# Self-attention of a perceiver block: PSUM in eight single banks taken in turn, scores of a head group in three parts

## The chip, the cores and the metric

The kernel runs on one core of a Trainium2 chip. The time is device microseconds (us) of one execution, as the median of several. The engines are TensorE (PE; its weight loads are shown as PEld), VectorE (DVE), ScalarE (ACT), GpSimd (POOL) and SyncE (SP, which issues DMAs). PSUM, where TensorE writes, has 8 banks of 128 partitions x 512 fp32.

## What is computed

Two batch elements of 512 tokens and 512 features pass through three residual layers: cross-attention over 8192 context rows, causal self-attention, and a mixture of 16 experts (two for each token). Only the self-attention is changed. All weights and activations are fp32. Cut to what matters:

```python
q_amp = softplus(x @ Wq_amp.T);  q_phi = pi * tanh(x @ Wq_phi.T)      # k_amp, k_phi alike; 16 heads of 32
q_amp = q_amp / sqrt(mean(q_amp**2) + eps)                            # per head and token; k alike
scores = (q_amp*cos(q_phi) @ (k_amp*cos(k_phi)).T
          + q_amp*sin(q_phi) @ (k_amp*sin(k_phi)).T) / sqrt(32) * exp(log_scale[head])
attn = softmax(where(causal, scores, -inf))
x = x + (attn @ v) @ Wo.T                                             # x was normalised before the projections
```

## The kernel before

The 16 heads go in NG = 4 groups of four; one group's channels fill 128 partitions, 32 to a head. Tokens are in TB = 4 blocks of P = 128. For each batch element b the kernel has, feature by token, `cs[b,i,u]` and `sn[b,i,u]` (amplitude times cosine and sine; i is 0 for queries and 1 for keys, u a pair of groups).

A score product of a group is, for each head, two fp32 matmuls (cosine and sine, `product`, L1093) that use only the head's 32 rows of TensorE, into a bank of the head's own; four heads, in four quarters of the rows, can run side by side. Each fp32 matmul shows as two instructions in the trace. Other shapes on TensorE: full 128 x 128 (projections, `channels`, L874), and column matmuls with 32 columns of weights for each head (values `weighted`, L1158, and sums `close`, L1188; `columns`, L158, does the same with a full weight cut into four).

Scores are made twice. `score_max` (L1101) makes them query by key for block qt, up to the diagonal; VectorE adds the causal mask to the diagonal block (L1108) and takes the row maxima (L1109). `split` writes the maxima as three bf16 parts (VectorE and POOL), and `max_rows` (L1119) turns them into rows with matmuls on an identity, which VectorE casts (L1130). `score_exp` (L1133) makes the scores key by query for key block kt, subtracts the maxima by a bf16 matmul with `sa.minus` (L1141), ScalarE takes the exponential (L1143), and POOL sets what lies above the diagonal to zero (L1145). `weighted` multiplies by the values, `close` sums the exponentials with a matrix of ones, and VectorE divides: it transposes the sums (L1193), takes the reciprocal, transposes back (L1199) and multiplies (L1200).

PSUM has two pools here: `ps` holds three pairs of banks (tag "s", 128 x 2 x 512), and `ps1` two single banks, "j" (projections, rows of maxima, sums, transposes, router) and "av" (values). So a part of scores for four heads takes two of the three pairs.

The order is written out by hand: instructions run on each engine in the order of the program. `attend(b, fill)` goes through the groups; in group g it makes the exponentials of key blocks x = 0 to 3 and, between them, the maxima of group g + 1 in the order of `ORDER` ([3], [2], [1, 0], []), the values of block x - 1, and in x = 0 the sums and the division of group g - 1. Other work is put at named gaps (`fill`, eight to a group and one after it): in `attend(0)` the amplitudes, logarithms, values and phases of batch element 1, cut into single matmuls; in `attend(1)` the second half of `combine` for element 1 and the pieces of `route(0)` (normalisation, transposes, router, ranks of tokens). `first_maxima(b)` makes the maxima of group 0 ahead of it; the four outputs of element 0 (`output`, L1246) stand at the start of `attend(1)`, those of element 1 after it.

Before the attention lies a preparation: values of element 0, the last output tiles of the cross-attention (`finish`, L158 and L482) with the statistics of the normalisation behind them on VectorE, four turns (transposes through bank "j", L142, copied by ScalarE, L143), the raw phases of element 1 (L874), `root` and `combine` for element 0. After it come the rest of `route`, the experts and the output.

The cross-attention ahead of all this already takes its eight PSUM banks singly and in turn.

Of the kernel before, what the change touches and what calls it, by code (L numbers as in the profile page):

```python
# [20 lines left out]
P = 128  # L21
# [21 lines left out]
def perceiver_kernel(ctx: ExitStack, tc: tile.TileContext, a, out: bass.AP):  # L43
# [91 lines left out]
    def turn(ps, pstag, src, dst, copy):  # L135

        if pstag == "s":
            pt = ps.tile([P, 2, 4, P], F32, tag=pstag, name="pt")[:, 0]
        else:
            pt = ps.tile([P, 4, P], F32, tag=pstag, name="pt")  # L140
        for c in range(4):
            nc.tensor.transpose(pt[:, c, :], src[:, c * P : (c + 1) * P], ident)  # L142
        copy(dst, pt)  # L143

    def layernorm(ps, pstag, b, xnT, keep=None):

        for i, xn in enumerate(norm_tiles(b, keep)):
            turn(ps, pstag, xn, xnT[:, :, i * P : (i + 1) * P], nc.scalar.copy)

    def by_chunk(t):  # L150

        return [t[:, c, :] for c in range(ND)]

# [14 lines left out]
    def cross_attention(tail):  # L168

        with ExitStack() as st:  # L170
            wp = st.enter_context(tc.tile_pool(name="xa_w", bufs=1))
            sm = st.enter_context(tc.tile_pool(name="xa_sm", bufs=2))

            ps = st.enter_context(tc.tile_pool(name="xa_ps", bufs=1, space=PSUM))
            turns = [0]

            def bank(at=None):

                if at is None:
                    at, turns[0] = turns[0], turns[0] + 1  # L180
                return ps.tile([P, S], F32, tag=f"s{at % 8}", name="s")
# [304 lines left out]
            def finish(b, ps, tag, qts, after=None):  # L486

                po = ps.tile([P, 2, D], F32, tag=tag, name="po")
                for k, qt in enumerate(qts):
                    finish_tile(b, acc, qt, po[:, k, :], after)  # L490

# [104 lines left out]
            return lambda ps, tag, after: [finish(B - 1, ps, tag, (qt, qt + 1), after) for qt in range(0, TB, 2)]  # L596
# [274 lines left out]
    def channels(pz, w, g, xT, cc=range(ND)):  # L871

        for c in cc:
            nc.tensor.matmul(pz, w[c][:, g * P : (g + 1) * P], xT[:, c, :], start=(c == 0), stop=(c == ND - 1))  # L874
# [12 lines left out]
    def xattn_tail(k):  # L887


        def channels(pz, w, g, xT):  # L890
            for c in range(ND):
                columns(pz, w[c][:, g * P : (g + 1) * P], xT[:, c, :], c == 0, c == ND - 1)
# [86 lines left out]
    def self_attention(finish_cross, mo_w):  # L979
        with ExitStack() as st:  # L980
            wp = st.enter_context(tc.tile_pool(name="sa_w", bufs=1))
            sm = st.enter_context(tc.tile_pool(name="sa_sm", bufs=2))
            ps = st.enter_context(tc.tile_pool(name="sa_ps", bufs=3, space=PSUM))
            ps1 = st.enter_context(tc.tile_pool(name="sa_ps1", bufs=1, space=PSUM))

            def values(b, h, copy):

                if h == 0:
                    vals[b] = b8("v", (P, TB, D))
                pv = ps.tile([P, 2, D], F32, tag="s", name="pv")  # L990
                for k in range(2):
                    i = 2 * h + k
                    for c in range(ND):
                        nc.tensor.matmul(  # L994
                            pv[:, k, :], xnT[b][:, c, i * P : (i + 1) * P], sa.wv[c], start=(c == 0), stop=(c == ND - 1)
                        )
                copy(vals[b][:, 2 * h : 2 * h + 2, :], pv)

            def value(b, i):

                pv = []

                def piece(c):
                    if c == 0:
                        pv.append(ps1.tile([P, D], F32, tag="j", name="pv"))
                    nc.tensor.matmul(
                        pv[0], xnT[b][:, c, i * P : (i + 1) * P], sa.wv[c], start=(c == 0), stop=(c == ND - 1)
                    )
                    if c == ND - 1:
                        nc.vector.tensor_copy(vals[b][:, i, :], pv[0])  # L1010

                return [lambda c=c: piece(c) for c in range(ND)]
# [17 lines left out]
            def root(b):  # L1030

                pq = ps1.tile([P, S], F32, tag="j", name="pss")
# [36 lines left out]
            def raw_phase(b, i, u):  # L1069
                pz = ps.tile([P, 2, S], F32, tag="s", name="pz")  # L1070
                for k in range(2):
                    channels(pz[:, k, :], sa.wphi[i], 2 * u + k, xnT[b])
                cs[b, i, u] = m4("phi")
                nc.scalar.copy(cs[b, i, u], pz)

            def combine(b, rs, i, u):

                pb = ps.tile([P, 2, S], F32, tag="s", name="pb")
                for k in range(2):
                    q = slice((2 * u + k) * HD, (2 * u + k + 1) * HD)  # L1080
                    nc.tensor.matmul(
                        pb[:, k, :], sa.back[q, i].rearrange("p j d -> p (j d)"), rs[q, :], start=True, stop=True
                    )
                z = amp[b, i, u]
                nc.vector.tensor_tensor(z, z, pb, ALU.mult)
# [3 lines left out]
            def product(s, b, g, j, own, lhs_at, other, rhs_at, stop):  # L1089

                r = slice(j * HD, (j + 1) * HD)
                for n, f in enumerate((cs, sn)):
                    nc.tensor.matmul(  # L1093
                        s,
                        f[b, own, g // 2][r, g % 2, lhs_at],
# [72 lines left out]
            def first_maxima(b):  # L1168
                oT[b] = b8("soT")
                cm = sm.tile([P, TB, 4], F32, tag="scm", name="scm")  # L1170
                for qts in ORDER:
                    for qt in qts:
                        score_max(b, 0, qt, cm)
# [260 lines left out]
```

## Time and profile before

| | us |
|---|---|
| median of 3 runs (lowest, highest) | 3122.87 (3122.15, 3124.74) |
| the profiled execution | 3127.96 |
| its span, first to last instruction | 3126.3 |
| TensorE busy in the span | 2967.6 (95%) |
| VectorE, ScalarE, POOL busy | 2024.2 (65%), 1384.2 (44%), 2168.0 (69%) |
| granted TensorE clock, mean | 0.971 |
| cross-attention | to about 2580 |
| self-attention with its preparation | 2580 to 2962 |
| rest of the route, experts, output | 2962 to 3126.3 |

A program's profile gives for each instruction its engine, its line of the kernel, start and length, and what ended an idle time before it ("<-DVE scm L1109": that VectorE instruction released it). A matmul's end is modelled, so busy time of TensorE includes matmuls that run slower than they could. The granted clock is the share of TensorE's full clock that the chip let through; it is given for windows of time.

### The profile page before, as it was taken

What the parts mean: (1) busy time and instruction counts of PE and PEld (TensorE: products, weight loads), DVE (VectorE), ACT (ScalarE), POOL (GpSimd) and SP (SyncE); (2) the same over time, 40 slices, a digit from 0 to 9 for tenths busy, and PEclk for the clock granted to TensorE, in tenths of its full rate; (3) what the DMA queues carried; (4) which work ended last, traced back from release to release, by engine and by line L of the source; (5) the groups of instructions that cost most, each with busy time, mean ns of one, the idle gap of its engine ahead of it and who ended that gap; (6) DMA issues with size and microseconds to landing.
All of it is one profiled execution on the core that took longest, in us unless ns stands there. A gap on an engine that the chain in (4) does not pass through costs nothing.

```text
span 3126.3 us, 62064 instructions
## 1 busy us (share of the span) xinstructions
PE 2967.6 (95%) x26687; PEld 1158.9 (37%) x26687; DVE 2024.2 (65%) x3337; ACT 1384.2 (44%) x2550; POOL 2168.0 (69%) x861
## 2 busy tenths in 40 slices
PE   7999999999999999999999999999999989889875
PEld 3333333333333333333333333333333323344464
DVE  2667776767777677756677776777777656465522
ACT  1345444555555555435555545555544454242211
POOL 1488989898988889968889888989887730010012
PEclk9999999999999999999999999999999999899878
DMA  3000000000000000000000000000000010010274
GB/s 138 1 3 15 10 15 10 23 1 23 4 21 8 16 8 17 15 16 15 10 15 10 15 10 15 10 15 3 2 1 28 28 52 17 1 48 28 89 244 147
DMA packets 47364, 89.51 MB, mean 29 GB/s; under 512 B 4320, under 2 KB 22768, under 8 KB 47088
## 3 DMA queue, kind: packets, MB, share of 16 engines
q1 hardware_dynamic: 39824, 69.26, 6.9%
q0 software_dynamic: 2784, 8.41, 0.9%
q10 hardware_dynamic: 4480, 7.87, 0.8%
q8 instruction: 209, 3.42, 0.5%
q14 instruction: 67, 0.55, 0.1%
HBM read 77.13 MB, written 8.39 MB: 27 GB/s over the span
## 4 chain that ended last, share of the span: by engine, by line
PE 90%; DVE 6%; DMA 1%; issue 1%; ACT 1%; POOL 0%; ACTq 0%; DVEq 0%; POOLq 0%
PE s L158 26%; PE s L375 17%; PE s L440 15%; PE s L388 14%; PE s L407 3%; PE p L1093 3%; PE pz L874 2%; PE ph L794 2%; PE s L467 2%; PE s L310 1%; PE spo L1246 1%; PE po L811 1%; DVE cm L397 1%; PE pv L994 1%; PE spa L1188 1%
## 5 line engine op out<-in xcount | busy, mean ns | idle before, releaser
L576 POOL TENSOR_TENSOR es<-es,e 128x2048 f32<-128x2048 f32 x374 | 1700.2, 4546 | 80.3 <-ACT e L409 63.3
L409 ACT ACTIVATE e<-s 128x512 f32<-128x512 f32 x2048 | 1057.5, 602 | 1116.3 <-PE s L407 1113.3
L397 DVE TENSOR_REDUCE cm<-s 128x1 f32<-128x512 f32 x2048 | 1270.9, 683 | 315.6 <-PE s L375 315.5
L375 PE MATMUL s<-k,qT 32*128 32x512 f32 x4096 | 591.4, 641 | 3.7 <-DVE cm L397 3.7
L388 PE MATMUL s<-qT,k 32*128 32x512 f32 x4096 | 555.6, 595 | 7.6 <-ACT e L409 6.8
L440 PE MATMUL s<-e,v 128*32 128x512 f32 x4096 | 498.2, 604 | 12.6 <-DVE cm L397 11.5
L576 POOL TENSOR_TENSOR es<-e 128x2048 f32<-128x2048 f32 x63 | 286.1, 4541 | 226.5 <-ACT e L409 226.5
L158 PE MATMUL s<-wkv,ctx 128*32 128x512 f32 x3072 | 369.9, 602 | 7.5 <-DVE cm L397 7.2
L158 PE MATMUL s<-ctx,wkv 128*32 128x512 f32 x3072 | 357.2, 599 | 3.5 <-DVE cm L397 3.1
L388 PEld LDWEIGHTS s<-qT,k 32*128 32x128 f32 x4096 | 282.8, 185 | 188.2 <-issue 104.1
L455 DVE TENSOR_TENSOR acc<-acc,s 128x512 f32<-128x512 f32 (+1 forms) x359 | 207.9, 604 | 141.0 <-PE s L440 140.4
L375 PEld LDWEIGHTS s<-k,qT 32*128 32x128 f32 x4096 | 164.7, 183 | 333.7 <-issue 256.9
L440 PEld LDWEIGHTS s<-e,v 128*32 128x32 f32 x4096 | 107.6, 109 | 333.6 <-DVE cm L397 171.6
L407 PE MATMUL s<-rows,mb 4*128 4x512 bf16 x2048 | 217.9, 377 | 0.0
L351 DVE SCALAR_TENSOR_TENSOR k<-s,kf,m 128x512 f32<-128x512 f32 x128 | 96.1, 751 | 177.8 <-PE s L158 177.8
L158 PEld LDWEIGHTS s<-ctx,wkv 128*32 128x32 f32 x3072 | 87.4, 110 | 239.3 <-issue 156.1
L158 PEld LDWEIGHTS s<-wkv,ctx 128*32 128x32 f32 x3072 | 87.2, 110 | 224.6 <-issue 130.4
L1145 POOL TENSOR_SCALAR_AFFINE_SELECT e<-e 128x512 f32<-128x512 f32 x32 | 22.0, 687 | 212.0 <-ACT e L1143 212.0
L366 ACT COPY v<-s 128x512 f32<-128x512 f32 x128 | 75.0, 586 | 119.8 <-PE s L158 96.8
L463 DVE TENSOR_TENSOR acc<-acc,s 128x1024 f32<-128x1024 f32 x56 | 68.4, 1221 | 69.9 <-ACT s L462 69.9
L407 PEld LDWEIGHTS <-mb 4*128 4x128 bf16 x2048 | 68.3, 93 | 106.2 <-issue 105.6
L1093 PE MATMUL p<-phi 32*128 32x384 f32 (+3 forms) x512 | 79.6, 521 | 13.1 <-DVE scm L1109 7.6
(261 smaller groups left out, 1909.6 us busy)
## 6 DMA issues: line engine op xcount, KB each, us to landing
ctx<-in_ctxT_dram SPq DMA_DIRECT2D x48, 512.0 KB, 3.7
wg<-in_L_ffn_w_gate_dram SPq DMA_DIRECT2D x16, 512.0 KB, 4.9
wf<-in_L_ffn_w_fc_dram SPq DMA_DIRECT2D x16, 512.0 KB, 5.6
wp<-in_L_ffn_w_proj_dram SPq DMA_DIRECT2D x16, 512.0 KB, 5.3
results<-res ACTq DMA_DIRECT2D x32, 128.0 KB, 3.4
xs<-in_x_dram SPq DMA_DIRECT2D x2, 1024.0 KB, 6.5
m<-in_mask_BxS_bf_dram SPq DMA_DIRECT2D x16, 128.0 KB, 3.1
w_wq_phiT<-in_wq_phiT_dram SPq DMA_DIRECT2D x2, 1024.0 KB, 5.1
```

The lines of the kernel that those rows point to most:

```text
L158: nc.tensor.matmul(out[q], lhsT[:, q], rhs, start=start, stop=stop)
L351: nc.vector.scalar_tensor_tensor(k[:, keys], bank, kf[:, g, b : b + 1], mask_tiles[i][:, keys], ALU.subtract, ALU.mult)
L366: nc.scalar.copy(v[:, kt % (NKT // 2), :], bank)
L375: nc.tensor.matmul(s, qT(chunks[i][0], g, r, slice(qt * P, (qt + 1) * P)), k_tiles[n][r, hf * S : (hf + 1) * S], start=True, stop=True,)
L388: nc.tensor.matmul(s, k_tiles[n][r, keys], qT(chunks[i][0], g, r, slice(0, S)), start=True, stop=False)
L397: nc.vector.tensor_reduce(cms[g][chunks[i][1] % 2][:, qt, j : j + 1, hf], ss[j], AX.X, ALU.max)
L407: nc.tensor.matmul(ss[j], bias_tiles[i][r4, keys], rows[r4, :], start=False, stop=True)
L409: nc.scalar.activation(e[:, j, :], ss[j], AF.Exp)
L440: nc.tensor.matmul(av[j * HD : (j + 1) * HD, :], v_tiles[i][kt // (NKT // 2)][:, kt % (NKT // 2), h * HD : (h + 1) * HD], e[:, j, :], star ...
L455: nc.vector.tensor_tensor(dst, dst, src, ALU.add)
L576: nc.gpsimd.tensor_tensor(es, first if kt == 1 else es, e, ALU.add)
L1093: nc.tensor.matmul(s, f[b, own, g // 2][r, g % 2, lhs_at], f[b, other, g // 2][r, g % 2, rhs_at], start=(n == 0), stop=stop and n == 1,)
```

## The change

- **PSUM.** The pools `ps` and `ps1` of the self-attention give way to one pool with eight tags, each a single bank, and `Ring` hands them out strictly in turn (0, 1, ... 7, 0, ...). Everything takes its bank there: scores, projections, values, sums, rows of maxima, transposes. The cross-attention's own counter becomes the same class.
- **Parts.** The scores of a group come in three parts of four banks: block 3 (512 columns), block 2 (384), and blocks 1 and 0 in the same bank (256 and 128 beside each other); so for the exponentials, with key blocks 0, 1, and 2 with 3. Causal add, maximum and exponential are one instruction per head in place of one per two heads. The matmuls of a part are written with the function (cosine, sine) outermost and the heads inside.
- **Order.** The maxima run four parts ahead of the exponentials (`AHEAD`), across groups, and stand next to them: maxima, exponentials, then other work. The values and sums of a group stand together after its third part, first blocks 0 and 1, then, after the next group's rows and a gap, blocks 2 and 3; the division follows at once.
- **Fills.** Projections, values and outputs are whole (16 column matmuls in a bank) and no longer cut into pieces; they have new places. Three amplitudes stand between the first four parts of maxima of element 0, three outputs between those of element 1. `tanh` and the first phases of element 1 stand on ScalarE ahead of `first_maxima(0)`.
- **Shapes and engines.** `channels`, `value`, `output` and `max_rows` use `columns` (four column matmuls in place of a full one). ScalarE copies the rows of maxima in place of VectorE. `raw_phase`, `combine` and the last output tiles of cross-attention go bank by bank.

The core of the diff:

```diff
+    class Ring:
+        def __init__(self, pool):
+            self.pool, self.n = pool, 0
+        def __call__(self, at=None):
+            if at is None:
+                at, self.n = self.n, self.n + 1
+            return self.pool.tile([P, S], F32, tag=f"s{at % 8}", name="s")
...
-            ps = st.enter_context(tc.tile_pool(name="sa_ps", bufs=3, space=PSUM))
-            ps1 = st.enter_context(tc.tile_pool(name="sa_ps1", bufs=1, space=PSUM))
+            bank = Ring(st.enter_context(tc.tile_pool(name="sa_ps", bufs=1, space=PSUM)))
...
-        for c in cc:
-            nc.tensor.matmul(pz, w[c][:, g * P : (g + 1) * P], xT[:, c, :], start=(c == 0), stop=(c == ND - 1))
+        for c in range(ND):
+            columns(pz, w[c][:, g * P : (g + 1) * P], xT[:, c, :], c == 0, c == ND - 1)
...
+            def product(ss, b, g, own, lhs_at, other, rhs_at, at):
                 for n, f in enumerate((cs, sn)):
+                    for j in range(4):
+                        r = slice(j * HD, (j + 1) * HD)
+                        nc.tensor.matmul(
+                            ss[j][:, at],
...
+            PARTS = 3
+            AHEAD = PARTS + 1
+            def score_max(b, n):
+                g, x = divmod(n, PARTS)
...
+                ss = [bank() for _ in range(4)]
+                if x < 2:
+                    qt = 3 - x
+                    w = (qt + 1) * P
+                    product(ss, b, g, 0, slice(qt * P, w), 1, slice(0, w), slice(0, w))
+                    for j, s in enumerate(ss):
+                        nc.vector.tensor_tensor(s[:, qt * P : w], s[:, qt * P : w], sa.causal, ALU.add)
+                        nc.vector.tensor_reduce(cm[:, qt, j : j + 1], s[:, :w], AX.X, ALU.max)
+                else:
+                    product(ss, b, g, 0, slice(P, 2 * P), 1, slice(0, 2 * P), slice(0, 2 * P))
+                    product(ss, b, g, 0, slice(0, P), 1, slice(0, P), slice(2 * P, 3 * P))
+                    for j, s in enumerate(ss):
+                        own = s[:, P : 3 * P].rearrange("p (a k) -> p a k", a=2)
+                        nc.vector.tensor_tensor(own, own, sa.causal.unsqueeze(1).to_broadcast([P, 2, P]), ALU.add)
+                        nc.vector.tensor_reduce(cm[:, 1, j : j + 1], s[:, : 2 * P], AX.X, ALU.max)
+                        nc.vector.tensor_reduce(cm[:, 0, j : j + 1], s[:, 2 * P : 3 * P], AX.X, ALU.max)
+                    split(g, top.pop(g))
...
+                nc.scalar.copy(rows, pr)
...
+            def score_exp(b, g, x, rows, e):
+                ss = [bank() for _ in range(4)]
+                w = 0
+                for kt in ([0], [1], [2, 3])[x]:
+                    at = slice(w, w + S - kt * P)
+                    product(ss, b, g, 1, slice(kt * P, (kt + 1) * P), 0, slice(kt * P, S), at)
+                    for j in range(4):
+                        q = slice(j * HD, j * HD + 3)
+                        nc.tensor.matmul(ss[j][:, at], sa.minus[q, :], rows[q, kt * P :], start=False, stop=True)
+                    w = at.stop
+                for j in range(4):
+                    nc.scalar.activation(e[:, j, :w], ss[j][:, :w], AF.Exp)
...
+            def first_maxima(b, *between):
+                for n in range(AHEAD):
+                    score_max(b, n)
+                    for f in between[n : n + 1]:
+                        f()
...
+                rows = max_rows(0)
+                for g in range(NG):
+                    for x in range(PARTS):
+                        gap(g, x, "rows")
+                        if PARTS * g + x + AHEAD < PARTS * NG:
+                            score_max(b, PARTS * g + x + AHEAD)
+                        score_exp(b, g, x, rows, (e0, e1, e23)[x])
+                        if x < 2:
+                            gap(g, x)
+                    av, pa = bank(), bank()
...
+                    for kts in ((0, 1), (2, 3)):
+                        for kt in kts:
+                            weighted(b, g, kt, es[kt], av)
+                        for kt in kts:
+                            sums(kt)
+                        if kts[0] == 0 and g + 1 < NG:
+                            rows = max_rows(g + 1)
+                        if kts[0] == 0:
+                            gap(g, "act")
+                            gap(g, 2)
...
+            phases(1, PAIRS[0:1])
+            first_maxima(0, *(lambda g=g: amplitude(1, 0, g) for g in range(3)))
+            put(0, 0, later(amplitude, 1, 0, 3))
+            put(0, 1, later(amplitude, 1, 1, 0))
+            put(0, "act", later(phases, 1, PAIRS[2:3]))
+            put(1, 0, later(amplitude, 1, 1, 1))
+            put(1, 1, later(amplitude, 1, 1, 2))
+            put(1, 1, later(amplitude, 1, 1, 3))
+            put(1, "act", lambda: [log_ln(1, p) for p in PAIRS])
+            for i in range(2):
+                put(2, i, later(value, 1, i, copy))
+                put(2, i, lambda i=i: [log_b(1, p) for p in PAIRS[2 * i : 2 * i + 2]])
+                put(3, i, later(value, 1, 2 + i, copy))
+            put(2, "act", roots)
+            put(3, 0, lambda: sa.newton())
+            for i in range(2):
+                put(3, i + 1, "rows", lambda i=i: combine(1, sa.rs, i, 0))
+            put(3, "act", later(phases, 1, [PAIRS[1], PAIRS[3]]))
...
+            first_maxima(1, *(lambda i=i: output(0, i) for i in range(3)))
+            put(0, 0, later(output, 0, 3))
+            for i in range(2):
+                put(0, i, "rows", lambda i=i: combine(1, sa.rs, i, 1))
```

In element 1 the twenty pieces of `route(0)` then stand one or two to a gap: statistics in group 0, the root and the normalised tiles in group 1, transposes and router in group 2, choice and ranks in group 3.

## The prediction

> **What bounds the kernel now.** Times are microseconds (us) unless marked. I first looked at the page's picture of the span in 40 slices (78 us each). These two rows are the busy tenths of TensorE (PE) and the clock that it was granted.
>
> ```profile
> PE   7999999999999999999999999999999989889875
> PEclk9999999999999999999999999999999999899878
> ```
>
> From slice 2 to 32 TensorE is full: that is cross-attention, which the change leaves alone. The self-attention is slices 34 to 38, where both rows dip. So I asked for windows: one of cross-attention, then the preparation, first half (batch element 0), second half (element 1) and last output of the self-attention, all of it, and what follows. The columns are length, busy time (instructions) of PE, weight load, DVE, ACT, POOL, then the granted clock.
>
> ```profile
> 1500.00:2500.00 1000.00, 987.05 (x9458) 355.67 (x9454) 700.35 (x1118) 494.23 (x944) 860.53 (x299) 0.99 0.04 13
> 2580.00:2653.00 73.00, 66.62 (x276) 26.10 (x280) 44.34 (x61) 31.38 (x34) 0.00 (x0) 0.98 0.05 15
> 2653.00:2824.00 171.00, 144.89 (x988) 66.05 (x983) 89.97 (x138) 67.02 (x83) 14.43 (x33) 0.88 0.11 35
> 2824.00:2948.00 124.00, 111.97 (x941) 61.24 (x938) 71.80 (x146) 28.50 (x42) 14.07 (x28) 0.89 0.13 42
> 2948.00:2962.00 14.00, 14.00 (x36) 5.91 (x32) 7.07 (x13) 0.00 (x0) 0.00 (x0) 1.00 0.14 49
> 2580.00:2962.00 382.00, 337.48 (x2230) 159.30 (x2230) 213.19 (x357) 126.89 (x158) 28.50 (x61) 0.91 0.11 34
> 2962.00:3126.30 164.30, 111.32 (x711) 92.64 (x710) 47.01 (x110) 20.91 (x40) 31.70 (x32) 0.80 0.61 192
> ```
>
> All that can change lies in 382 us. TensorE has work in 88% of them, but at a clock of 0.91, and busy time overstates it, as the timeline of TensorE shows. First a score product that finds all its banks free, then one that doesn't (start, length, engine and line, instructions; a product is two fp32 matmuls per head, each two instructions):
>
> ```profile
> 2764.88 1.16 PE L1093 MATMUL p<-phi 32*128 32x512 f32 x8
> 2765.84 1.06 PE L1093 MATMUL p<-sn 32*128 32x512 f32 x8
> 2766.70 0.42 PE L1141 MATMUL p<-rows,s_minus 3*128 3x512 bf16 x4
> ...
> 2654.49 0.91 PE L1093 MATMUL p<-phi 32*128 32x384 f32 x4
> 2655.14 0.91 PE L1093 MATMUL p<-sn 32*128 32x384 f32 x4
> 2656.56 0.92 PE L1093 MATMUL p<-phi 32*128 32x384 f32 x4 [0.51 <-DVE scm L1109]
> 2657.28 0.85 PE L1093 MATMUL p<-sn 32*128 32x384 f32 x4
> ```
>
> The reader is to see that the first does four heads of 512 columns in 1.82 (2766.70 - 2764.88). The second, a quarter narrower, runs two heads, waits for VectorE to free a pair of banks, and runs the other two: 3.64 (to 2658.13), for work that side by side would take 1.82 x 3/4 = 1.37. Two heads take as long as four, and the row calls that busy. The same answer, asked for the product's line alone, has it busy 60.61 in the first half and 62.89 in the second, **123.5 together**. The third loss is the single bank "j", through which each projection, row of maxima and sum must pass:
>
> ```profile
> 2679.65 0.40 PE L1141 MATMUL p<-rows,s_minus 3*128 3x512 bf16 x4 [2.84 <-DVE rows L1130]
> 2727.66 3.78 PE L874 MATMUL pz<-sxnT,w_wk_ampT 128*128 128x512 f32 x4 [4.62 <-DVE amp L882]
> ```
>
> In the second, TensorE stands 4.62 behind a copy that VectorE reaches only after two maxima and the division of a group.
>
> **The change, part by part.** Let me call the halves II (171) and III (124): 295 = 123.5 of products + 133.4 of other busy TensorE (144.89 + 111.97 - 123.5) + 38.1 idle.
>
> *Products.* Four single banks per part let the four heads run together unless a bank is late. Per group of four heads, at full clock: 512 columns 1.72 (1.82 less 0.1 for the turn from column to row matmuls), 384 columns 1.3 (three quarters), 256 columns 0.96 (the undisturbed one at 2746.3), 128 columns 0.88 (two heads take 0.44 at 2747.26, where the weight loads set the pace). Sum 4.9, for maxima and exponentials 9.8, times 8 groups: **78** in place of 123.5.
>
> *Other matmuls.* Full 128 x 128 matmuls become four column matmuls. Four chunks take 3.64 in columns (the po rows of L158) and 7.13 / 2 = 3.56 full (L874), so the 16 projections in II and III cost 0.1 each, 1.6, against fewer turns between shapes, since a projection is no longer cut into pieces between row matmuls and sums stand beside values. I set the two equal. Bounds: 3 lost, or 5 gained if the turns (0.1 each, perhaps fifty fewer by the code) all count. What changes is the clock: 133.4 at 0.885 is **118** at full speed.
>
> *VectorE.* Its maxima are now per head. 512 columns take 1.225 for two heads in 1024 elements and 0.692 for 512, so 0.16 of each is fixed. A part of 512 costs 4 x (0.29 + 0.69) = 3.9, of 384 3.4, of 256 and 128 together 4 x (0.425 + 0.42 + 0.29) = 4.6. The widths 128 (0.29, causal add) and 384 (0.56, reduction) have no row; 0.28 to 0.425 and 0.424 to 0.692 bound them, and I take the line through the rows. That is 11.9 a group against 10.0, 15 us in all; the casts of rows (8 x 0.69) go to ScalarE, so VectorE has 162 + 15 - 5.5 = 172 beside TensorE's 196. ScalarE's exponentials become 4 x 0.59 for 512 and 8 x 0.48 (between 0.38 and 0.59), 6.3 a group against 5.6, with room: 67 of 171.
>
> *Waits that come.* Banks are taken strictly in turn, so a part of maxima reuses the eight before it, and TensorE can be about one part ahead of VectorE. That is enough where a projection of 3.6 stands between the parts. Where it isn't:
> (a) At each group's end, the next exponentials need the bank of the values, free after two transposes, the reciprocal and the product, 0.72 + 0.24 + 0.71 + 0.69 = 2.4, with 1.4 of maxima as cover; and the last values wait for exponentials and two masks of 0.64 on POOL, some 0.6 beyond the sums. 1.6 x 8 = 13.
> (b) The four bursts of logarithm pieces (0.68 + 1.24 + 1.22, with rectifiers of 0.42, up to 4 us) sit in VectorE's queue ahead of maxima: about 2 each, 8.
> (c) In III few projections stand between parts, while two combinations (0.69 x 2 + 2.45 = 3.8 each) and the route's statistics, with a square root on ScalarE behind a table load of 1.28, come on VectorE: 7.7 + 2.5 and some smaller, 13.
> (d) At the start of an element, the first rows wait for three parts of maxima (12) and, for element 0, a burst behind ScalarE's phases: 5 + 4.
> Sum **43**, no less than the 38 of today. Bounds: 13, if (a) alone stays, and 75, if all that I called covered shows.
>
> *Clock.* Half speed is granted after waits: between 2660 and 2670 the clock was 0.66 with no wait over 0.51 just before, but with heads in pairs. Today it takes 0.09 x 382 = 34. With as many idle microseconds but denser products I put **14** (eight stretches of 3.4 at half, as 0.83 in a window of 10 stands for one). Bounds: 5 and 34.
>
> The skill's TensorE: Matmul & The Clock Gate, section "A second HAM failure mode: psum-queue depth-cycling", says that going through PSUM banks in each iteration makes short idle times after which the clock falls again and again, which speaks against this change. Here the cross-attention, which takes eight banks in turn, has 0.99, and the stretch with pairs of banks 0.91; by the rule the 34 would stay, and the sum would come out 20 higher.
>
> *Preparation.* The waits between two output tiles of cross-attention in one pair (0.81 and 2.02) go, but VectorE's chain to the normalised tiles behind them is as long, so that is no gain yet. The four turns, now each waiting for the copy before (1.33 apart in one bank), overlap: the last normalised tile is there at 2610.9, the last copy at about 2612.6 and not 2617.2. That is 4.7, and the stretch at 0.84 clock around 2616 goes, 1.7: **6.4**. Bounds: 2 and 10.
>
> *After the attention* (output 14, route and experts 164) the instructions are the same: nothing, plus or minus 3, by when the last statistics come. The loads of the experts' weights on SP are issued as before, and wait there for buffers.
>
> **Sum.** II and III: 78 + 118 + 43 + 14 = 253 against 295, -42; with the preparation -48.4. The profiled execution took 3127.96 (its span 3126.3): 3079.6. Runs without a profile have a median of 3122.87, so **3074**.
>
> **Rivals.**
> *The dense case.* If the banks work as in cross-attention (TensorE busy 99%, clock 0.99), only (a) and 5 of clock are left: 78 + 118 + 13 + 5 = 214, -81, with preparation -87: 3036. For it: the same ring runs at 99% there. Against: there VectorE is busy 70% with no bursts; here 172 of 239.
> *VectorE sets the pace.* Banks of maxima come free 0.98 apart (0.29 + 0.69), and a product of four heads needs four. If that splits the heads in a third of the products, they take 78 + 45 / 3 = 93, and the clock keeps 30: 93 + 118 + 43 + 30 = 284, -11, with the preparation -17: 3105. For it: VectorE's 11.9 a group in parts against TensorE's 11 for parts, where nothing fills. If nearly all are split, the change doesn't do what it says: 123.5 x 0.885 = 109, and 109 + 118 + 43 + 34 = 304 is +9, less the preparation's 6.4: no change.
> *Slower.* TensorE and VectorE take turns. A strict order means that a projection's bank can be held by a maximum that stands behind a logarithm burst, so everything after it waits. TensorE has 196, VectorE 172; the point is where the waits and the clock exceed 295 + 6.4 - 196 = 105 together, as with 80 of VectorE's 172 exposed and 25 of clock; at 100 exposed and 30 it is +25, 3148. For it: half clock and waits feed each other. Against: 38 of 162 are exposed now, with a single bank for all the fills.
>
> **Chances.** Forecast 0.55 (3052 to 3092), dense 0.15 (down to 3030), VectorE's pace 0.19 (3092 to 3116), within 0.2% of 3123 0.03, slower 0.08. About 0.2% (6 us) is what a measurement of this kernel can tell from no change. The range takes the forecast, its bounds of waits and clock, and most of the two neighbours: 3032 to 3108.
>
> **What would show it.** Products: the score rows come as x8 pairs with no wait inside, some 80 us in II and III. Waits: few on copies of projections; those left name the values' division and the maxima of the part before. The clock of the attention rises from 0.885 to some 0.95. The preparation ends near 2646. It is wrong if products are still split in x4, if VectorE is over 85% busy in III, or if the time after the last output moves by more than 5.

## The result and the profile after

The changed kernel takes 3074.86 (3074.22 to 3076.08, 4 runs) against 3122.72 (3122.15 to 3124.74) for the kernel before: **ratio 0.9846, 95% interval 0.983 to 0.9861**, 47.9 us less; the forecast was 3074, 48.4 less. The profiled executions are 3127.96 and 3074.43, their spans 3126.3 and 3072.4: 53.9 less. The two differences are 6 apart since the profiled execution of the kernel before is a long one: in experiment 9 this kernel has 3122.24 to 3129.65, and both of its executions with a trace (3127.96 and 3129.65) are at the upper end. No trace shows where an execution of 3122 is shorter.

The same two rows of the page as before the change:

```profile
PE   7999999999999999999999999999998998989875
PEclk9999999999999999999999999999999999999988
```

The span is cut into 40 slices again, of 77 us; the clock's dips in the self-attention are gone from the picture (a 9 stands for 0.9 or more), that of the experts at its end stays. The same stretches as windows, columns as before: cross-attention, preparation, first half (II), second half (III), last output, all of the self-attention, and what follows.

```profile
1500.00:2500.00 1000.00, 987.05 (x9461) 355.78 (x9456) 699.80 (x1118) 494.10 (x944) 860.45 (x300) 0.99 0.04 13
2580.00:2645.00 65.00, 63.05 (x561) 19.73 (x562) 44.17 (x64) 32.05 (x39) 0.00 (x0) 1.00 0.05 16
2645.00:2784.00 139.00, 119.14 (x1308) 50.77 (x1304) 89.93 (x181) 66.09 (x100) 14.66 (x33) 0.93 0.09 29
2784.00:2895.00 111.00, 102.57 (x1113) 56.49 (x1106) 76.00 (x195) 36.08 (x67) 13.15 (x28) 0.93 0.21 71
2895.00:2909.70 14.70, 14.61 (x136) 4.30 (x128) 7.09 (x14) 0.00 (x0) 0.00 (x0) 0.96 0.01 2
2580.00:2909.70 329.70, 299.37 (x3094) 131.30 (x3094) 217.19 (x454) 134.21 (x205) 27.82 (x61) 0.94 0.12 39
2909.70:3072.40 162.70, 107.25 (x710) 89.79 (x710) 46.86 (x110) 20.91 (x40) 31.64 (x32) 0.82 0.62 194
```

The self-attention went from 382 to 329.7, the preparation from 73 to 65, II from 171 to 139, III from 124 to 111. The score products alone (line 1062 of the changed kernel), II and III:

```profile
2645.00:2784.00 139.00, 48.11 (x512) 27.02 (x512) 0.93 0.09 29
2784.00:2895.00 111.00, 59.72 (x512) 35.18 (x512) 0.93 0.21 71
```

So II and III, 250 in all, are 107.8 of products + 113.9 of other busy TensorE (119.14 + 102.57 - 107.8) + 28.3 idle. Before: 123.5 + 133.4 + 38.1.

What a product looks like now, in the timeline of TensorE: first the maxima of block 3 with all banks free, then, from 2819.71 on, the maxima of block 3 of another group in III.

```profile
2644.99 1.14 PE L1062 MATMUL s<-phi 32*128 32x512 f32 x8
2645.96 1.04 PE L1062 MATMUL s<-sn 32*128 32x512 f32 x8
2646.92 3.64 PE L166 MATMUL s<-sxnT,w_wq_ampT 128*32 128x512 f32 x32
...
2819.71 4.21 PE L1062 MATMUL s<-phi 32*128 32x512 f32 x6 [1.75 <-DVE scm L1097]
2822.70 1.22 PE L1062 MATMUL s<-sn 32*128 32x512 f32 x2
2822.72 1.06 PE L1062 MATMUL s<-phi 32*128 32x512 f32 x1
2823.57 1.06 PE L1062 MATMUL s<-sn 32*128 32x512 f32 x1
```

The first takes 1.93 (2646.92 - 2644.99) for four heads; a part of 384 columns takes 1.51 and the part of 256 with 128 columns 1.52, read in the same way at 2650.49 and 2655.57. The second counts as busy from 2819.71 on, but its heads start one by one, as VectorE's maxima free their banks. Two of their weight loads (PEld) show it, 1.0 apart:

```profile
2820.71 0.29 PEld L1062 LDWEIGHTS s<-phi 32*128 32x128 f32 x2 [0.71 <-DVE scm L1097]
2821.70 0.50 PEld L1062 LDWEIGHTS s<-phi 32*128 32x128 f32 x2 [0.70 <-DVE scm L1097]
```

The waits on copies out of bank "j" are gone. The longest that TensorE has left in II are these:

```profile
2682.44 1.93 PE L166 MATMUL s<-sxnT,w_wk_ampT 128*32 128x512 f32 x8 [3.40 <-DVE scm L1097]
2711.85 1.86 PE L166 MATMUL s<-sxnT,w_wk_ampT 128*32 128x512 f32 x8 [3.41 <-DVE scm L1097]
2728.63 2.22 PE L1144 MATMUL s<-e,v 128*32 128x512 f32 x12 [4.60 <-DVE scm L1089]
2769.41 0.70 PE L1052 MATMUL s<-rs,back 32*128 32x512 f32 x2 [3.41 <-DVE rs L1023]
```

Three wait for maxima that stand in VectorE's queue behind a burst of logarithm pieces, the fourth for the root of element 1 (`newton`).

### The profile page after: what moved, and what is told of

It is laid out like the page before. It is cut to its first block, busy times and chain, and to the rows that moved or that the text cites. A ratio compares the mean times of both kernels' runs of the same rounds, so it can differ in the third digit from the quotient of the medians.

```text
span 3072.4 us, 63904 instructions
## 1 busy us (share of the span) xinstructions
PE 2925.5 (95%) x27551; PEld 1128.2 (37%) x27551; DVE 2027.4 (66%) x3434; ACT 1391.5 (45%) x2597; POOL 2167.0 (71%) x861
## 4 chain that ended last, share of the span: by engine, by line
PE 90%; DVE 6%; ACT 1%; DMA 1%; issue 1%; POOL 0%; ACTq 0%; POOLq 0%; DVEq 0%
PE s L166 30%; PE s L375 17%; PE s L440 16%; PE s L388 14%; PE s L407 3%; PE ph L788 2%; PE s L1062 2%; PE s L467 2%; PE s L310 1%; PE po L805 1%; DVE cm L397 1%; PE s L1144 1%; PE s L1183 1%; DMA wq<-in_L_xattn_Wq_dram 1%; DVE acc L476 1%
## 5 line engine op out<-in xcount | busy, mean ns | idle before, releaser
L440 PE MATMUL s<-e,v 128*32 128x512 f32 x4096 | 498.1, 604 | 12.6 <-DVE cm L397 11.4
```

Source lines behind the costliest of these rows:

```text
L440: nc.tensor.matmul(av[j * HD : (j + 1) * HD, :], v_tiles[i][kt // (NKT // 2)][:, kt % (NKT // 2), h * HD : (h + 1) * HD], e[:, j, :], star ...
```

## The experiments

All runs in one table; how to read it: SA is the self-attention from the first matmul of the values to the end of the last output, the products and TensorE's idle time are those of II and III, all from one trace each. The ratio is that of the medians against the kernel before on the same chip. Each of the two kernels has two traces, and SA repeats to 0.2 in them (329.7 and 329.6 for the changed kernel, 382 and 381.8 for the kernel before), so I take a difference of 1 or more between two profiles as real; the medians are compared within a chip only. For experiments 1, 2, 7 and 10, whose sets of runs don't hold the changed kernel, the interval of the ratio overlaps those of the changed kernel (0.9846 and 0.9829): what they are worth stands on SA alone.

| kernel | median | ratio [95%] | SA | products | idle | clock in SA |
|---|---|---|---|---|---|---|
| before, again | 3127.86 | 1.0002 [0.9992, 1.0011] | 381.8 | 123.7 | 38.2 | 0.91 |
| changed, again | 3064.93 | 0.9829 [0.9813, 0.9846] | 329.6 | 107.8 | 28.3 | 0.94 |
| 1 full matmuls | 3072.16 | 0.9855 [0.9839, 0.9872] | 333.4 | 107.4 | 27.5 | 0.94 |
| 2 heads outermost | 3072.64 | 0.9856 [0.984, 0.9873] | 334.0 | 111.2 | 25.0 | 0.94 |
| 3 single banks, old order | 3126.09 | 1.003 [1.0019, 1.0042] | 391.6 | 141.2 | 33.6 | 0.89 |
| 4 the same with two "j" | 3144.92 | 1.006 [1.0043, 1.0077] | 395.8 | 159.8 | 22.1 | 0.87 |
| 5 new order, pairs of banks | 3081.77 | 0.9884 [0.9868, 0.9901] | 346.3 | 102.1 | 40.7 | 0.91 |
| 6 maxima three parts ahead | 3069.67 | 0.9844 [0.9828, 0.9861] | 332.1 | 101.6 | 32.6 | 0.93 |
| 7 logarithms later | 3062.29 | 0.9825 [0.9809, 0.9842] | 323.4 | 112.6 | 19.4 | 0.94 |
| 8 the same, `combine` later | 3055.98 | 0.9798 [0.9782, 0.9814] | 319.4 | 110.0 | 16.8 | 0.94 |
| 10 rows cast by VectorE | 3077.85 | 0.9843 [0.9826, 0.9859] | 332.5 | 107.4 | 28.8 | 0.94 |
| 11 no causal add | 3061.03 | 0.9799 [0.9783, 0.9816] | 316.5 | 99.8 | 22.7 | 0.95 |

My theory after the result was that the gain comes from the banks (four heads side by side, no single "j"), with the new order needed for a part of it. The rival was that the order makes it, and shapes and banks are secondary.

**1. Full matmuls.** The changed kernel with full 128 x 128 matmuls where it has column matmuls (`channels`, `value`, `output`, `max_rows`):

```diff
-            columns(pz, w[c][:, g * P : (g + 1) * P], xT[:, c, :], c == 0, c == ND - 1)
+            nc.tensor.matmul(pz, w[c][:, g * P : (g + 1) * P], xT[:, c, :], start=(c == 0), stop=(c == ND - 1))
```

> The changed kernel with projections, values, outputs and rows of maxima as full 128 x 128 matmuls again, all else as changed. My theory (banks taken singly and an order that lets four heads run side by side): 3075 within 4, since 32 projections of 3.64 in columns against 3.56 full are 2.6, and a full matmul turns the array from rows as a column matmul does. Rival (the shapes were the gain, since full, row and column matmuls no longer alternate): 3090 or more.

SA 333.4, 3.8 more than the changed kernel's 329.6, with products and clock as there: in II and III the other busy time is 117.5 (224.8 - 107.4) and not 113.9. So the columns are worth 3.8 of the 52.

**2. Heads outermost.** The order of the eight matmul pairs of a part, head by head as before the change:

```diff
-                for n, f in enumerate((cs, sn)):
-                    for j in range(4):
+                for j in range(4):
+                    for n, f in enumerate((cs, sn)):
```

> The changed kernel with the loop over heads outermost in the score product again (cosine and sine of a head one after the other), all else as changed. My theory: 3075 within 3, since the trace of before shows four heads side by side (x8, x8) under that order of the loops whenever banks were free. Rival (the order of the loops lets the heads run together): products of 108 us become some 150 and the time 3110.

SA 334.0, 4.4 more; products 111.2 against 107.8. Small as well.

**3. Single banks in the order of before.** The kernel before with six single banks in place of three pairs, "j" and "av" kept; causal add, maximum, exponential, copies and `combine` go bank by bank. Nothing else moves:

```diff
-            ps = st.enter_context(tc.tile_pool(name="sa_ps", bufs=3, space=PSUM))
+            ps = st.enter_context(tc.tile_pool(name="sa_ps", bufs=6, space=PSUM))
...
-                tiles = [ps.tile([P, 2, S], F32, tag="s", name="p1") for _ in range(2)]
+                tiles = [ps.tile([P, S], F32, tag="s", name="p1") for _ in range(4)]
```

> The kernel before, in its own order and with its banks j and av, but with the three pairs of banks as six single banks (maxima and exponentials one instruction per head). My theory (both are needed: single banks, and an order in which parts, values and projections do not pass through one bank): a third of the gain, 3107 within 8. Rival A (the single banks are the gain): 3085 or less. Rival B (the order and the bank j are all of it): 3123 within 4, or slower by the added VectorE instructions.

Slower than before: SA 391.6 against 381.8. My theory fell here. VectorE has 16 more in SA (228.8 against 212.8), and the products take more, not less.

**4. The same with two banks "j".** It was still possible that single banks lose only through the one bank "j". Five banks for scores, two for "j":

```diff
-            ps = st.enter_context(tc.tile_pool(name="sa_ps", bufs=6, space=PSUM))
+            ps = st.enter_context(tc.tile_pool(name="sa_ps", bufs=5, space=PSUM))
...
+                    return few_banks.tile(shape, dtype, tag=tag, name=name, bufs=2 if tag == "j" else 1)
```

> The kernel before in its own order with single banks, as in the run of single banks alone (self-attention 391.6, 1.003 of the kernel before), but five of them in the s pool and two for j, where that run had six and one. If the one bank j, through which projections, rows and sums pass, is what held the single banks back, its waits (5.11 behind the copies of the amplitudes, 2.84 twice behind the rows) go and the self-attention falls by 10 to 20, to 372 to 382, at or below the 381.7 of the kernel before. Rival: the old order asks for a score bank of each head before the maxima of the last part are through, whatever j does, and with one bank fewer in that pool it gets no shorter than 388: then the split heads are the loss and j only where some of the waits show.

The rival holds: idle time falls by 11.5, products rise by 18.6, SA is 395.8. Two things change at once here, a bank more for "j" and one fewer for scores. The timeline shows how the products lose; these are the maxima of block 2, with no other work between two parts:

```profile
2648.12 0.48 PE L1097 MATMUL p<-sn 32*128 32x384 f32 x1
2648.30 0.58 PE L1097 MATMUL p<-phi 32*128 32x384 f32 x1
2648.44 0.48 PE L1097 MATMUL p<-sn 32*128 32x384 f32 x1
2648.73 0.48 PE L1097 MATMUL p<-phi 32*128 32x384 f32 x1
2649.05 0.48 PE L1097 MATMUL p<-sn 32*128 32x384 f32 x1
```

The heads start one by one, each as VectorE frees a bank. This part takes 4.7 (2646.10 to 2650.78), all of it busy by the rows, where the changed kernel takes 1.51. The clock falls right behind it, to 0.51 from 2652 to 2662, and TensorE counts as busy without a break from 2640 on. Where parts of maxima follow each other, single banks give VectorE's pace, and VectorE is slower by single heads.

**5. The new order with pairs of banks.** The changed kernel with four pairs in turn; maxima and exponentials by two heads as before the change, and a projection, rows or values with sums take a pair each:

```diff
-                ss = [bank() for _ in range(4)]
+                two = [bank.pair() for _ in range(2)]
+                ss = [two[j // 2][:, j % 2, :] for j in range(4)]
...
-                for j in range(4):
-                    nc.scalar.activation(e[:, j, :w], ss[j][:, :w], AF.Exp)
+                for p, s in enumerate(two):
+                    nc.scalar.activation(e[:, 2 * p : 2 * p + 2, :w], s[:, :, :w], AF.Exp)
```

> The changed order with a ring of four pairs of banks in place of eight single banks: maxima and exponentials again one instruction for two heads, a projection takes a pair and uses half, values and sums share one. Theory after the last set (the order is the gain, and single banks are what gives it room): half of the gain lost, 20 to 30 more than the changed kernel. Rival A (the order alone is the gain): within 5 of the changed kernel or faster, since VectorE has 15 us less to do. Rival B (neither does anything without the other): as slow as the kernel before, within 8.

SA 346.3: 35.5 below the kernel before, 16.7 above the changed one, less than the 20 to 30 of the theory and more than rival A has. TensorE's idle time is longer, 40.7 against 28.3, and the clock lower, 0.91:

```profile
2681.59 5.93 PE L166 MATMUL s<-sxnT,w_wk_ampT 128*32 128x512 f32 x32 [4.32 <-issue]
2711.93 9.56 PE L166 MATMUL s<-sxnT,w_wk_ampT 128*32 128x512 f32 x64 [4.37 <-DVE scm L1118]
2730.04 3.21 PE L1166 MATMUL s<-e,v 128*32 128x512 f32 x16 [5.15 <-DVE scm L1108]
```

With 3 this is a square: old order 381.8 with pairs and 391.6 with singles, new order 346.3 and 329.6. **Single banks cost 10 in the old order and save 17 in the new.** The 35.5 that the rest of the change is worth with pairs hold the preparation (7), and, if they add up, shapes, loop order and rows (3.8, 4.4 and 2.9 by experiments 1, 2 and 10); that leaves some 17. That they add up wasn't tried. "New order" stands here for all the rest of the change: the 17 hold the order, the whole fills, the three parts and the one ring of eight banks for everything, and no run takes these apart; the ring wasn't tried in the old order.

More than half of the two differences is clock. Take TensorE's busy time in II and III times what the clock lacks, summed over windows of 1 us: 30.3 for the kernel before, 36.9 in experiment 3, 47.6 in experiment 4, 27.5 here and 17.5 for the changed kernel. II and III are 11.0 longer in experiment 3 than before, 6.6 of them clock, and 16.4 longer here than in the changed kernel, 10.0 of them clock.

**6. Maxima three parts ahead** in place of four (`AHEAD = PARTS`):

> The changed kernel with the maxima three parts ahead of the exponentials and not four, all else as changed. Theory (the fourth part gives VectorE and POOL the time to turn a group's maxima into rows): the rows of a group wait for a part of 4.6 on VectorE and 1.3 on POOL with some 5 us of TensorE as cover, 1 to 2 more per group, 8 to 15 in all. Rival (the distance doesn't matter once the banks go round): within 3.

SA 332.1, 2.5 more; the median 4.7 above the changed kernel's on that chip. Products are 6 shorter, but the first rows stand right behind the maxima they need:

```profile
2665.20 0.62 PE L166 MATMUL s<-identb,parts 128*32 128x128 bf16 x16 [5.62 <-POOL parts L1106]
```

Between the two by the medians (4.7; theory 8 to 15, rival within 3), at the rival by SA: in II and III the fourth part ahead saves 4.3 of waits and 3.7 of other matmuls, and the products give back 6.3 of it.

**7. Logarithms later.** The four bursts of rectifiers and `log_a` leave their place right after an amplitude and go one gap further:

```diff
-                if g % 2:
-                    for f in relu:
-                        f()
-                    relu.clear()
-                    log_a(b, (i, g // 2))
...
+            put(0, 1, later(logs, 1, 0, 1))
+            put(1, 1, later(logs, 1, 1, 0))
+            put(1, "act", later(logs, 1, 1, 1))
```

> The changed kernel with VectorE's bursts of rectifier and logarithm pieces put behind the next part's maxima instead of ahead of them; the same instructions. My theory (what TensorE still waits for is a bank whose maximum stands behind a burst): the waits of 3.40, 3.41 and 4.60 in the first half go for the most part, and with them half-speed stretches: 8 to 14 less, 3064. Rival (VectorE's total work binds, wherever it stands): 3075 within 3.

SA 323.4, 6.2 less, short of the theory's 8 to 14 but not the rival's nothing. The waits of 3.40, 3.41 and 4.60 are gone; three of 1.75, 1.76 and 2.14 stand in their place, the last one on the division of a group:

```profile
2664.41 1.52 PE L1062 MATMUL s<-phi 32*128 32x384 f32 x3 [1.75 <-DVE amp L876]
2688.53 0.48 PE L1062 MATMUL s<-phi 32*128 32x256 f32 x1 [1.76 <-DVE amp L876]
2727.64 1.23 PE L1062 MATMUL s<-phi 32*128 32x512 f32 x3 [2.14 <-DVE soT L1208]
```

**8. And `combine` later:** 7, and the first two combinations of element 1 both stand ahead of group 3's third part, where one stood ahead of its second, right behind the root's chain.

```diff
-                put(3, i + 1, "rows", lambda i=i: combine(1, sa.rs, i, 0))
+                put(3, 2, "rows", lambda i=i: combine(1, sa.rs, i, 0))
```

> The late logarithm bursts, and the two combinations of the last group of element 0 both put before its third part, so that the first no longer waits for VectorE's root. Theory (the wait of 3.41 on the root and the half speed after it are on the path): 3 to 5 less than the late bursts alone, 0.981 of the kernel before. Rival (the two combinations, 3.8 of VectorE each, then stand ahead of element 1's first maxima and give it back): within 1.5 of the late bursts alone, 0.9825.

SA 319.4, 4.0 below experiment 7: the wait of 3.41 for the root is gone. 3055.98 is 8.95 below the changed kernel on the same chip, and the fastest kernel of the study that leaves nothing out.

**9. Both kernels once more.**

> The changed kernel itself, once more, as the yardstick of this set of runs (the kernel before took 3117 and not 3123 in the last set): 0.9846 of the kernel before, within 0.0015.

> The kernel before once more, for a second trace of it. The self-attention should take 381.7 as in the first trace, within 1, and the time after the last output 154 to 156, not the 164.1 of the first trace, since the changed kernel's went from 162.8 to 155.1 between two chips with its self-attention the same. Then the 53.9 between the two profiled spans and the 47.9 between the medians differ by what lies outside the self-attention. If the self-attention moves by more than 2, stage times can't be compared between chips as done here.

The self-attention repeats (329.6 and 381.8). The ratio of the changed kernel is 0.9829, 0.0017 from 0.9846, just outside the 0.0015 expected. What follows the self-attention doesn't repeat: 155.1 for the changed kernel here, 162.7 in its first trace, and 165.5 for the kernel before, against the 154 to 156 that I expected of it. The last window of the changed kernel, then of the kernel before, columns as above (the last one is GB/s):

```profile
2908.20:3063.30 155.10, 104.49 (x714) 87.97 (x710) 46.82 (x110) 20.77 (x40) 31.84 (x32) 0.83 0.64 204
```

```profile
2962.40:3127.90 165.50, 111.20 (x710) 93.14 (x710) 47.01 (x110) 20.91 (x40) 32.12 (x32) 0.80 0.61 191
```

It doesn't go with the change: on the two chips of experiments 1 to 8 (without 4) every kernel has 153 to 157, in the other traces 162 to 166. Each chip had one set of runs, so chip and set can't be told apart, and nothing was tried on why. The kernel before has 3122.24 to 3129.65 on one chip, so its first profiled execution, 3127.96 beside a median of 3122.72, is within its own spread.

**10. Rows cast by VectorE.**

```diff
-                nc.scalar.copy(rows, pr)
+                nc.vector.tensor_copy(rows, pr)
```

> The changed kernel with the eight casts of the rows of maxima on VectorE, as before the change, and not on ScalarE. If VectorE's load sets the pace of banks, 8 x 0.69 = 5.5 more on it and its place in the queue behind maxima lengthen the self-attention (329.6) by 2 to 6. Rival: ScalarE is the engine that the values wait for, through the exponentials, so the cast is better on VectorE: shorter by up to 3. Nothing within 1 would mean that this part of the change is worth nothing.

SA 332.5, 2.9 more, within the 2 to 6: moving 5.5 off VectorE was worth half of that.

**11. No causal add.** The forecast's term that failed is the products (next section). The test: take VectorE's causal additions away, 32.2 us, so that banks come free sooner.

```diff
-                        nc.vector.tensor_tensor(s[:, qt * P : w], s[:, qt * P : w], sa.causal, ALU.add)
...
-                        nc.vector.tensor_tensor(own, own, sa.causal.unsqueeze(1).to_broadcast([P, 2, P]), ALU.add)
```

> The changed kernel without the additions of the causal mask ahead of the maxima: 64 of 0.291 and 32 of 0.424, 32 us of VectorE, are left out, so a row's maximum also runs over the later keys of its diagonal block (the exponentials are masked after it as before). The bank of a head then comes free 0.69 after the last and not 0.98. If VectorE's pace of freeing banks is what spreads the four heads of a product and keeps the products at 107.8 where 78 were forecast, the products fall to 85 to 98 and the self-attention (329.6) by 12 to 25, to 305 to 318. Rival A: the spread comes from ScalarE's exponentials, 0.48 to 0.59 a head in the same ring of banks; then the products stay above 103 and the self-attention falls only by the waits on maxima, 3 to 8. Rival B: the row of products counts as busy what overlaps anyway, and a product costs what it must; then products and self-attention stay within 3.

SA 316.5, 13.1 less, inside the 12 to 25; products 99.8, between the theory's 85 to 98 and A's 103. So the causal additions alone, a third of VectorE's work on the parts, account for 8 of the products' excess (107.8 - 99.8), and for 5.6 of the idle time. Rival B is out. What holds the products at 99.8 and not at 79 isn't settled: VectorE's maxima are still there, and I took nothing from ScalarE's exponentials, which share the ring.

## Why the prediction was right, and where it wasn't

The sum held: II and III -45 (253 forecast, 250 measured), the preparation -8, together 53 from trace to trace where 48.4 were forecast, and 47.9 between the medians. That it came so close is in part luck, since its terms were wrong in opposite directions: busy TensorE in II and III took 221.7 where 210 were forecast (78 + 118 and 14 of clock), and idle time 28.3 where 43 were.

- **Products: 78 forecast, 107.8 measured. This is the step that failed:** "Four single banks per part let the four heads run together unless a bank is late." The price of a group's parts with all banks free held in its sum, each part being off by 0.2 to 0.3: 1.93 + 1.51 + 1.52 = 4.96 against 4.86 (1.72 + 1.3 + 0.96 + 0.88), so 79 for all sixteen. But banks are late often, in III above all (59.7, where II has 48.1), and a late bank delays a head and not the part, so the loss stands inside busy time. The rival "VectorE sets the pace" named the mechanism and put it at 93. About 10 of the 29 are half clock (the products' busy time times what the clock lacks, over windows of 0.5), which my sum counted elsewhere. The sign that I had named, score rows as x8 pairs, didn't come: rows of x8 hold 57% of the products' instructions in the timeline of II and III, and 58% before.
- **Waits: 43 forecast, 28.3 measured.** (b), the bursts: 8 forecast, 3.40 + 3.41 + 4.60 = 11.4 seen, 6.2 by experiment 7. (c): 13 forecast; the root's 3.41 and, in III, waits of 1.75, 1.62 and 1.07 on maxima and 2.27 on the route (`whose`, L741) are 10.1. (a), group ends, 13: no wait over 1 us names the division or POOL's masks, and the short ones on the division add up to 2; only when the bursts move does one of 2.14 on the division appear. (d), 9: 2.28 before the first rows. What I summed as waits came back as split heads: waits and products together were forecast at 121 and are 136.
- **Other matmuls: 118 forecast, 113.9 measured.** I had set columns and full matmuls equal, bounds 3 lost to 5 gained; experiment 1 gives the columns 3.8 over the whole self-attention.
- **VectorE: 172 forecast, 165.9 measured** in II and III (89.93 + 76.00). The widths without a row held: 0.291 for the causal add of 128 columns and 0.558 for the reduction of 384, where I had 0.29 and 0.56, and causal additions and maxima together went from 80.0 to 94.7, the 15 of the forecast. The other 6 are overlap: added up row by row VectorE went from 169.5 to 178.8, close to the 9.5 forecast (15 - 5.5), but busy time counts overlapping rows once, and the many short rows overlap by 12.9 where the rows before overlapped by 7.7.
- **Clock: 14 forecast, 20 measured** (0.06 x 329.7), from 34. The trace has it inside the busy terms above, so these would be lower with the clock apart, as in my sum. Eight stretches of 3.4 at half clock were forecast; in II and III, by windows of 1 us, eight came, three of them of 6.8.
- **Preparation: -6.4 forecast, -8 measured;** the first score product starts at 2644.99 (2646 forecast), and the last copy of the turns ends at 2611.5 (2612.6 forecast, 2617.2 before). That bank "j" was the cause fits experiments 3 and 4: the preparation takes 71.3 with one "j" and 66.1 with two.
- **After the attention: 0 plus or minus 3;** 14 + 164.3 became 14.7 + 162.7, a change smaller than the 7.6 by which this part differs between two traces of the changed kernel.
- **What the prediction didn't see** is the split of the gain between banks and order. It priced the single banks as the cause and the order as a source of waits. By experiments 3 to 5 the banks save nothing without the rest of the change. As I read the timelines, what keeps heads together is that a projection, values or sums stand between two parts of maxima, while VectorE empties the last ones; no run changes that alone.

The rivals: the dense case (3036) isn't reached even with no causal add (3061.03) or with bursts and combinations moved (3055.98). The slower one came true for the banks without the order, 1.003 [1.0019, 1.0042] and, with two "j", 1.006 [1.0043, 1.0077], though not through its mechanism: there, heads are taken one by one.

## What to carry to other kernels

Splitting PSUM into single banks paid here only together with the rest of the change; as the timelines read, it needs an order that puts other TensorE work between two groups of results that the same engine must empty. Without it the smaller instructions, slower in sum, set the pace, the clock falls, and the split costs time. Read a row-tiled matmul's busy time against its undisturbed length: heads that start one by one look busy. And when one wait is removed, look for its place in the next term (here products took 29 more than forecast where waits took 15 less), and add the two before believing either.

## What the hardware showed

- Half clock needs no long wait of TensorE. In these two windows of 10 us the clock is 1.00 and then 0.66, and TensorE was idle for 1.93 in the first, 1.75 of it the wait before 2819.71 shown above:

```profile
2810.00:2820.00 10.00, 8.07 (x89) 4.17 (x90) 8.05 (x16) 3.97 (x9) 0.64 (x1) 1.00 0.01 2
2820.00:2830.00 10.00, 10.00 (x72) 6.21 (x74) 9.26 (x24) 1.23 (x4) 1.30 (x4) 0.66 0.01 2
```

  The second has TensorE busy throughout, with few heads at a time. The Trainium skill, in TensorE: Matmul & The Clock Gate, section "Why this matters for your kernels", gives the rule of no idle gap over some 3 us between bursts of matmuls; here a wait of 1.75 with heads one by one behind it was enough. In experiment 4 there is no wait at all: TensorE counts as busy in all of 2640 to 2662, with heads one by one from 2646 to 2656, and the clock is 1.00 up to 2652 and 0.51 from there to 2662. So such a thin stretch can do it alone; what part the wait of 1.75 had isn't settled.
- The same page's "A second HAM failure mode: psum-queue depth-cycling" tells of a kernel whose clock went up and down as it cycled through PSUM banks. Here the eight banks in turn have a clock of 0.94 in the self-attention, the four pairs in the same order 0.91, the old pools 0.91, and the cross-attention, eight in turn as well, 0.99: going through single banks in turn did not lower the clock. No run here is without such a cycle.
- The time after the self-attention differs by 7.6 between two traces of the changed kernel (155.1 and 162.7), at 204 and 194 GB/s, while 329.6 and 329.7 ahead of it are the same.
